# Graph layers on one core: three scatters to a slot, earlier SA loads, both message halves in one PSUM tile, later reloads of h

## Chip, core and metric

One NeuronCore of a Trainium2 chip runs one program. The metric is the device time of one execution in microseconds; several executions of a kernel are taken and their median is compared. Engines are named as in the profile: PE is TensorE (PEld its weight loads), DVE VectorE, ACT ScalarE, POOL GpSimd, SP SyncE. SP, ACT and POOL also issue DMAs; all of them run on the core's 16 DMA engines.

## What is computed

Two graph layers for 16 batches of 1024 nodes with 256 features, all in float32. `adj` is a 1024x1024 matrix with few nonzero edges.

```python
# layer 0, for each batch (feats = data @ W1.T, f1 = feats @ W2 + b2)
coefs = softmax(leaky_relu(f1[:, :, None] + f1[:, None, :]) + adj, axis=-1)
h = coefs @ feats + bias2 + data
# layer 1
hidden = relu(h @ W1u at u + h @ W1v at v + b1)        # for each pair u, v
S = sigmoid(hidden @ w2 + b2)                          # B x 1024 x 1024
a = einsum('buv,bud->bvd', S * adj, h)
m = einsum('uv,bud->bvd', adj, h) * h
z = beta1 * h + beta2 * (a @ Wa + ba) + beta3 * (m @ Wm + bm)
```

Where `adj` is zero, S is not needed. So the kernel computes S for the edges alone.

## The kernel before

**Dense part.** For each batch the attention of layer 0 gives h. From h come the two ends of an edge's hidden vector, `pu` and `pw` (tables in DRAM of 272 columns to a batch), the product `ha` = h Wa (DRAM), and the message branch: `message` (L1162) multiplies h by `adj` for one half of the nodes (512) and one half of the features (128, index h), 8 matmuls of 128x512 on a one-bank PSUM tile; `keep_message` (L1173) multiplies that on DVE by h transposed (`hT`) into `mT`; `product` (L1180) multiplies `mT` by Wm for two chunks of 128 nodes; `keep_product` (L1192) adds beta1 h into `zb`, and `store_product` (L1198) stores `zb` to DRAM from ACT's queue. Eight batches (LATER = 0, 1, 2, 3, 11, 12, 13, 14) put this branch off: their h goes to DRAM (`put_off`) and comes back through `take_up` (L1156), an SP load of 1 MB into one of three buffers `xh`; `turned_ends` then transposes h again on PE (`ph`), and ACT copies it to `hT`.

**Score part.** The batches are split into three groups with index 0, 1, 2 of 5, 5 and 6 batches. Each goes through 135 slots of 128 edges. `fetch` gathers a slot's rows of `pw` (tile `gv`) and, at the first slot of a table tile, of `pu` (tile `gu`) by indirect DMAs from POOL; `compare` (L1248) makes two DVE operations of it; `sums` (L1263) adds up each batch's 272 columns on ACT (every eighth slot of group 2 on DVE); after 16 slots ACT and DVE make the gates (`lg`), and each slot's gates are scattered to `sa_d` in DRAM by one more indirect DMA from POOL (`scatter`, L1232). Scatters whose gates are ready wait in the list `late`; `first` (L1283), at the head of every slot, fetches the slot some places ahead and then issues one or two scatters from that list. Group 0 and 1 have five buffers `gv`, group 2 has six of its own.

**Gather part.** When all of a group's scatters are done, `load_sa` (L1333) loads pieces of its `sa_d` on SP (tile `sat`, 7 buffers), ACT turns each round (`part_sa`, tile `apart`, 4 buffers), DVE multiplies it by `adj` (`weigh_sa`, L1354), and PE multiplies it by `ha` (`gather`, L1361, tiles `pzg` and `pzh`). `load_zb` brings `zb` back, DVE adds, ACT's queue stores the result. The groups are gathered in the order 1, 0, 2. So while group 2 is scored, PE does first what is left of the put-off messages and then the gathering of groups 1 and 0; group 2 is gathered at the end.

**Order.** No scheduler decides it: every step is put into a `Timetable` with a planned time (`times.at`; `times.matmuls` also advances the PE clock of the plan), and the steps are emitted in the order of those times. Each engine works through its own stream in that order and stops at the first instruction that must wait. DMAs of SP and ACT together use eight completion counters in turn, POOL's DMAs eight others: before a DMA is issued, its queue waits until the DMA eight places earlier in the same series has landed.

The put-off messages stand in a loop from L1617: seven times one `messages(..., 1)`, transposes, `messages(..., 0)`, two `product`s, so that `message`, `ph` and `pz` tiles all take turns in the four one-bank PSUM buffers `p1`; the two two-bank buffers `p2` are free meanwhile.

Of the kernel before, what the change touches and what calls it, by code (L numbers as in the profile page):

```python
# [8 lines left out]
F32 = mybir.dt.float32  # L9
AF = mybir.ActivationFunctionType  # L10
ALU = mybir.AluOpType
# [3 lines left out]
P = 128  # L15
BANK = 512
# [17 lines left out]
LATER = (0, 1, 2, 3, 11, 12, 13, 14)  # L34
# [337 lines left out]
def edge_layers(  # L372
# [36 lines left out]
    nc = tc.nc  # L409
    B, N, D = x.shape  # L410
    C = N // P
    H = D // P
    NG = len(GROUPS)
# [8 lines left out]
    p2 = ctx.enter_context(tc.tile_pool(name="p2", bufs=2, space=PSUM))  # L422
# [5 lines left out]
    adj_sb = const.tile([P, C, N], F32, name="adj_sb")  # L428
# [4 lines left out]
    dense = ctx.enter_context(tc.tile_pool(name="dense", bufs=1))  # L433
# [5 lines left out]
    held = {}  # L439
# [73 lines left out]
    for i in range(H):  # L513
# [5 lines left out]
        for o in range(H):  # L519
            nc.tensor.matmul(  # L520
                pw[:, :1],
                lhsT=w1_in[:, o, i * P : (i + 1) * P],
                rhs=w2_col0[:, o, :],
                start=(o == 0),
                stop=(o == H - 1),
# [397 lines left out]
    st = {}  # L923
# [232 lines left out]
    def take_up(b):  # L1156
        held[b] = dense.tile([P, C, D], F32, name="xh", bufs=3)
        nc.sync.dma_start(out=held[b].rearrange("p c d -> p (c d)"), in_=h_d[b])


    def message(b, half, h):
        span = slice(half * BANK, (half + 1) * BANK)  # L1162
        pm = st["pm", h] = p1.tile([P, BANK], F32, tag="p1", name="pm")
        for c in range(C):
# [5 lines left out]
                stop=(c == C - 1),  # L1170
            )

    def keep_message(b, half, h):  # L1173
        if h == 0:
            st["mT"] = dense.tile([P, H, BANK], F32, name="mT")
        nc.vector.tensor_tensor(
            st["mT"][:, h, :], st.pop(("pm", h)), st["hT", b, half][:, h, :], ALU.mult
        )
# [30 lines left out]
    PARTS = [16, 32, 48, 64, 80, 96, 112, 124, 131, len(SLOTS)]  # L1209
    AHEAD = [n - 2 for n in GV]  # L1210
    HA = 8
    SA = 7
    late = []

    def fetch(g, k):
        t, s = SLOTS[k]
        if s == 0:
            gu = st["gu", t] = pools["gath", g].tile([P, SIZE[g] * R], F32, name="gu", bufs=2)
            nc.gpsimd.indirect_dma_start(
                out=gu,  # L1220
                out_offset=None,
                in_=pu_d[g],
                in_offset=bass.IndirectOffsetOnAxis(ap=key_u[:, t : t + 1], axis=0),
            )
        gv = st["gv", k] = pools["gath", g].tile([P, SIZE[g] * R], F32, name="gv", bufs=GV[g])
        nc.gpsimd.indirect_dma_start(  # L1226
            out=gv,
            out_offset=None,
            in_=pw_d[g],
            in_offset=bass.IndirectOffsetOnAxis(ap=idx_v[:, t, s : s + 1], axis=0),  # L1230
        )

    def scatter(g, lg, i, k):
        t, s = SLOTS[k]
        dma = nc.gpsimd.indirect_dma_start(  # L1235
            out=sa_d[g],
            out_offset=bass.IndirectOffsetOnAxis(ap=idx_s[:, t, s : s + 1], axis=0),
            in_=lg[:, i, : SIZE[g]],
            in_offset=None,
            bounds_check=N * N - 1,  # L1240
            oob_is_err=False,
        )
        tc.declare_no_dep(dma.ins, group=f"sa{g}", reason="edges of their own")
        tc.add_to_no_dep_group(f"sa{g}", dma.ins)
# [4 lines left out]
    def compare(k, half):  # L1249
        if k in [0, *PARTS] and half == 0:  # L1250
            st["lg"] = dense.tile([P, PARTS[0], MOST], F32, name="lg", bufs=5)
        cols, op = ((slice(0, HALF), ALU.max), (slice(HALF, R), ALU.min))[half]
        mv = by_batch(st["gv", k])[:, :, cols]
        mu = by_batch(st["gu", SLOTS[k][0]])[:, :, cols]
        nc.vector.tensor_tensor(mv, mv, mu, op)  # L1255

    def place_of(k):

        part = next(i for i, end in enumerate(PARTS) if k < end)
        return (PARTS[part - 1] if part else 0), PARTS[part]  # L1260

    def sums(k, js, lg):
        one = by_batch(st["gv", k])  # L1263
        i = k - place_of(k)[0]
        if len(js) == one.shape[1]:
            nc.vector.tensor_reduce(lg[:, i, : len(js)], one, AX.X, ALU.add)
        else:
            for j in js:
                nc.scalar.activation(  # L1269
                    one[:, j, :], one[:, j, :], AF.Copy, accum_out=lg[:, i, j : j + 1]  # L1270
                )
# [7 lines left out]
    def scores(g, start, end, on_vector):  # L1279

        for k in range(len(SLOTS)):
            time = start + k * (end - start) / len(SLOTS)

            def first(k=k):
                for n in range(AHEAD[g]) if k == 0 else ():
                    fetch(g, n)
                if k + AHEAD[g] < len(SLOTS):
                    fetch(g, k + AHEAD[g])
                for _ in range(min(len(late), 2 if len(late) > PARTS[0] - 4 else 1)):
                    late.pop(0)()  # L1290

            def last(k=k):
                k0, k1 = place_of(k)
                lg = st["lg", k0]
                part = lg[:, : k1 - k0, : SIZE[g]]
                nc.vector.tensor_scalar(part, part, 1.0, None, ALU.add)
                late.extend(lambda i=i: scatter(g, lg, i, k0 + i) for i in range(k1 - k0))

            times.at(time - (15.0 if k == 0 else 0.0), first)
            times.at(time + 0.1, lambda k=k: compare(k, 0))  # L1300
            times.at(time + 0.9, lambda k=k: compare(k, 1))
            k0, k1 = place_of(k)
            if k == k0:
                times.at(time + 0.2, lambda k0=k0: st.update({("lg", k0): st["lg"]}))
            summed = lambda js, k=k, k0=k0: sums(k, js, st["lg", k0])
            if on_vector(k):
                times.at(time + 1.7, lambda f=summed: f(range(SIZE[g])))
            else:
                for j in range(SIZE[g]):
                    times.at(time + 2.0 + 0.6 * j, lambda f=summed, j=j: f((j,)))  # L1310
            if k + 1 == k1:
                times.at(time + 5.4, lambda k=k, k0=k0: gates(g, k, st["lg", k0]))
                times.at(time + 6.0, last)
        ended = end + 4.0
        if g + 1 == NG:
            times.at(ended, lambda: [late.pop(0)() for _ in range(len(late))])
        return ended
# [124 lines left out]
    def turned_ends(b, i):  # L1442
        end = times.matmuls(4 * P, lambda: turn_h(b, i))
        times.at(end + 0.3, lambda: keep_hT(b, i))
# [14 lines left out]
    def messages(b, half, h, delay=0.3):  # L1459
        time = times.matmuls(C * BANK, lambda: message(b, half, h))  # L1460
        times.at(time + delay, lambda: keep_message(b, half, h))

    def products(b, *ids):
        for i in ids:
            time = times.matmuls(4 * D, lambda i=i: product(b, i))
            times.at(time + 0.3, lambda i=i: keep_product(b, i))
            times.at(time + 2.3, lambda i=i: store_product(b, i))
        return time + 1.0

    times = Timetable()  # L1470
# [144 lines left out]
    times.at(lead - 0.5, check)  # L1615
    times.at(lead - 0.4, turn_over)
    messages(B - 1, 0, 1)  # L1617
    messages(B - 1, 1, 0, 3.8)
    products(B - 1, 0, 1)
    b = B - 1  # L1620
    for n in range(3):
        messages(b, 1, 1)
        turned_ends(LATER[n], 0)
        turned_ends(LATER[n], 1)
        messages(LATER[n], 0, 0, 3.8)
        time = products(b, 2, 3)
        b = LATER[n]
        times.at(time + 1.0, lambda b=LATER[n + 2]: take_up(b))
        messages(b, 0, 1)
        turned_ends(b, 2)  # L1630
        turned_ends(b, 3)
        messages(b, 1, 0, 3.8)
        products(b, 0, 1)
    messages(b, 1, 1)


    order = [*range(1, NG - 1), 0, NG - 1]
# [21 lines left out]
    for i, at in starts.items():  # L1659
        if i == 5:  # L1660
            continue
        b = LATER[i]
# [6 lines left out]
    when = []  # L1669
    begins = {}  # L1670
# [17 lines left out]
    due = when[last] - 30.0  # L1688
# [22 lines left out]
    )  # L1711
    for i, at in starts.items():
        if i + 2 < len(LATER):
            times.at(when[at] + 2.0, lambda b=LATER[i + 2]: take_up(b))
    times.at(when[starts[6]] + 2.0, load_rest)
    for n, (g, c) in enumerate((g, c) for g in order for c in range(C)):
        if n < C:
            due = opened + 2.0 + (when[0] - 14.0 - opened) * n / C
        elif n < HA:
            due = when[2 + n - C] + 0.1  # L1720
        else:
            k, c1 = divmod(n - HA, C)
            due = begins[order[k], C - 1, c1] + 2.4
        times.at(due, lambda g=g, c=c: load_ha(g, c))
    parts = list(begins)
    for i, p in enumerate(parts):
        due = when[0] - 36.0 + 4.0 * i if i < SA else begins[parts[i - SA]] - 4.0
        if p[0] + 1 == NG:
            due = max(due, ended + 0.1 + 0.01 * i)
        times.at(due, lambda p=p: load_sa(*p))  # L1730
        times.at(begins[p] - 8.2, lambda p=p: part_sa(*p))
        times.at(begins[p] - 6.0, lambda p=p: weigh_sa(*p))
    for i, (g, vc, half) in enumerate(halves):
        if half == 0:
            due = when[0] - 20.0 + 8.0 * i if i < 4 else when[i - 2] + 13.0
            if g + 1 == NG:
                due = max(due, ended + 0.2)
# [62 lines left out]
```

## Time and profile before

| | us |
|---|---|
| runs | 2083.23, 2078.31, 2081.45 (median 2081.45) |
| the profiled execution, its own time | 2079.83 |
| its span, first to last instruction | 2078.1 |
| PE busy | 2020.4 (97%) |
| DVE busy | 1566.8 (75%) |
| ACT busy | 1371.5 (66%) |
| POOL busy | 1142.4 (55%) |
| TensorE clock granted, mean | 0.994 |

The time is 1.7 us more than the span. All times given as places below are microseconds from the span's start. The put-off messages of the loop run from 1279 to 1416; PE then gathers groups 1 and 0 until 1904 and group 2 until 2069. POOL's last scatter stands at 1891. "Busy" PE is matmuls in the pipeline; idle time is what is left.

### The profile page before, as it was taken

Reading aid. Unit: us, or ns where it says so; the run is one execution under the profiler, and the core shown is the slowest. Engines: PE = TensorE matmul, PEld = TensorE weight load, DVE = VectorE, ACT = ScalarE, POOL = GpSimd, SP = SyncE. Lnnn points to the kernel's source line nnn. Section 1 sums busy time; section 2 is a strip of 40 time slices with the busy share of each in tenths; the row PEclk is TensorE's granted clock in tenths of the full one; section 3 lists DMA queues with packets and bytes.
Section 4 is the critical chain, followed back from the end, with each engine's and each line's share of the span. In section 5 each row is a group of like instructions: output and inputs, shape, how many; then the busy total and the mean of one; then the engine's idle time right before and its main releaser. Section 6 shows DMA issues by size and latency. Waiting matters only on the chain.

```text
span 2078.1 us, 28958 instructions
## 1 busy us (share of the span) xinstructions
PE 2020.4 (97%) x8577; PEld 1554.9 (75%) x8577; DVE 1566.8 (75%) x2348; ACT 1371.5 (66%) x4842; POOL 1142.4 (55%) x974
## 2 busy tenths in 40 slices
PE   8999999999999999999999999899999999999998
PEld 6888887777786868677888886457677667767887
DVE  7798883677777777677878886578888888884554
ACT  4212222577777868587888777577888888885654
POOL 1121221267676777677777777666777677683000
PEclk9999999999999999999999999999999999999999
DMA  6689886788888889789999999999999999996873
GB/s 220 240 311 343 306 323 235 247 268 288 285 273 270 275 288 297 254 299 308 315 297 318 327 308 310 326 401 399 399 400 370 415 414 405 400 383 254 281 230 123
DMA packets 250007, 644.37 MB, mean 310 GB/s; under 512 B 38642, under 2 KB 139762, under 8 KB 247794
## 3 DMA queue, kind: packets, MB, share of 16 engines
q0 software_dynamic: 82016, 348.87, 47.9%
q1 hardware_dynamic: 132002, 259.36, 34.2%
q10 hardware_dynamic: 35824, 34.22, 4.7%
q8 instruction: 69, 1.13, 0.2%
q14 instruction: 96, 0.79, 0.1%
HBM read 479.56 MB, written 162.92 MB: 309 GB/s over the span
## 4 chain that ended last, share of the span: by engine, by line
PE 61%; DVE 11%; DMA 9%; ACT 8%; issue 7%; POOL 3%; ACTq 0%; POOLq 0%; DVEq 0%
PE pv L1067 18%; PE pp L1105 10%; PE pm L1165 10%; PE pzg L1370 6%; DMA gv<-pw_d,idx_v 5%; ACT gv L1269 5%; PE pf L1013 5%; DVE gv L1255 4%; PE pea L1133 4%; PE pzh L1370 3%; PE pz L1185 2%; ACT apart L1352 2%; POOL sa_d L1235 2%; DMA xh<-in_x_dram 1%; POOL gv L1226 1%
## 5 line engine op out<-in xcount | busy, mean ns | idle before, releaser
L1269 ACT ACTIVATE gv<-gv 128x272 f32<-128x272 f32 x2058 | 856.3, 420 | 313.0 <-DVE gv L1255 204.7
L1255 DVE TENSOR_TENSOR gv<-gv,gu 128x680 f32<-128x680 f32 (+1 forms) x810 | 705.8, 909 | 97.5 <-DMA gv<-pw_d,idx_v 95.5
L1226 POOL DMA_INDIRECT gv<-pw_d,idx_v x405 | 497.1, 1227 | 297.9 <-ACT gv L1269 181.5
L1235 POOL DMA_INDIRECT sa_d<-lg,idx_s x405 | 504.1, 1245 | 135.2 <-issue 108.2
L1067 PE MATMUL pv<-feats,eT 128*128 128x257 f32 x2048 | 465.5, 380 | 2.7 <-DVE eT L1054 2.0
L1165 PE MATMUL pm<-adj_sb,xh 128*128 128x512 f32 x1024 | 452.8, 595 | 2.6 <-DVE xh L1081 2.6
L1067 PEld LDWEIGHTS pv<-feats,eT 128*128 128x128 f32 x2048 | 382.9, 190 | 61.8 <-DVE eT L1054 4.2
L1269 ACT ACTIVATION_READ_ACCUMULATOR gv<-gv 128x1 f32 x2058 | 389.7, 189 | 0.0
L1370 PE MATMUL pzg<-ha_g,apart 128*128 128x256 f32 x1536 | 367.5, 382 | 19.0 <-DVE apart L1357 18.5
L1165 PEld LDWEIGHTS pm<-adj_sb,xh 128*128 128x128 f32 x1024 | 194.3, 191 | 222.4 <-issue 219.8
L1370 PEld LDWEIGHTS pzg<-ha_g,apart 128*128 128x128 f32 x1536 | 290.2, 191 | 77.2 <-DVE apart L1357 29.5
L1352 ACT COPY apart<-sat 128x640 f32<-128x640 f32 (+1 forms) x192 | 264.2, 1394 | 78.0 <-PE pzh L1370 35.5
L1357 DVE TENSOR_TENSOR apart<-apart,adj_sb 128x640 f32<-128x640 f32 (+1 forms) x192 | 165.9, 867 | 123.3 <-ACT apart L1352 123.0
L1105 PE MATMUL pp<-wuv,hT 128*128 128x272 f32 x1024 | 250.5, 395 | 6.7 <-ACT end L1119 3.8
L1105 PEld LDWEIGHTS pp<-wuv,hT 128*128 128x128 f32 x1024 | 194.7, 191 | 53.7 <-issue 6.5
L1054 DVE SCALAR_TENSOR_TENSOR eT<-row,col,grown 128x512 f32<-128x512 f32 x256 | 182.8, 745 | 27.5 <-ACT col L1000 26.8
L852 POOL DMA_INDIRECT table_d<-rec,at x52 | 57.4, 1105 | 248.4 <-DVE rec L845 151.8
L1098 ACT COPY hT<-ph 128x512 f32<-128x512 f32 x96 | 55.1, 575 | 101.0 <-PE ph L1087 100.7
L1133 PE MATMUL pea<-wa,hT 128*128 128x256 f32 x512 | 121.0, 379 | 0.0
L1185 PE MATMUL pz<-wm,mT 128*128 128x256 f32 x512 | 115.7, 379 | 0.0
L1013 PE MATMUL pf<-w1T,xT 128*128 128x257 f32 x512 | 114.1, 380 | 0.9 <-DVE xT L971 0.9
L1370 PE MATMUL pzh<-ha_g,apart 128*128 128x256 f32 x384 | 114.2, 379 | 0.0
(179 smaller groups left out, 1589.0 us busy)
## 6 DMA issues: line engine op xcount, KB each, us to landing
sa_d<-zero SPq DMA_DIRECT2D x128, 512.0 KB, 5.6
sat<-sa_d SPq DMA_DIRECT2D x128, 320.0 KB, 9.5
sat<-sa_d SPq DMA_DIRECT2D x64, 384.0 KB, 4.2
pu_d<-end SPq DMA_DIRECT2D x64, 272.0 KB, 4.3
pw_d<-end SPq DMA_DIRECT2D x64, 272.0 KB, 5.8
ha_d<-ea SPq DMA_DIRECT2D x64, 256.0 KB, 4.9
zb_d<-zb ACTq DMA_DIRECT2D x64, 256.0 KB, 7.8
xh<-in_x_dram SPq DMA_DIRECT2D x15, 1024.0 KB, 13.6
```

The costliest lines, as they stand in the source:

```text
L1013: nc.tensor.matmul(pfs[i], lhsT=st["xT"][:, h, c * P : (c + 1) * P], rhs=w1T[:, h, :], start=(h == 0), stop=(h == H - 1),)
L1054: nc.vector.scalar_tensor_tensor(st["eT", b, k, n][:, i, :], st["row"][:, cols], st["col"][:, j : j + 1], grown[:, j, cols], ALU.max, ALU. ...
L1067: nc.tensor.matmul(pv[:, : D + 1], lhsT=st["eT", b, k, j // 4][:, j % 4, i * P : (i + 1) * P], rhs=st["feats", b][:, j, :], start=(j == 0) ...
L1105: nc.tensor.matmul(pp[:, k, :R], lhsT=st["hTi", b, i][:, h, k * P : (k + 1) * P], rhs=wuv[:, side, h, :], start=(h == 0), stop=(h == H - 1),)
L1133: nc.tensor.matmul(pp[:, k, :], lhsT=st["hTi", b, i][:, h, k * P : (k + 1) * P], rhs=wa[:, h, :], start=(h == 0), stop=(h == H - 1),)
L1165: nc.tensor.matmul(pm, lhsT=held[b][:, c, h * P : (h + 1) * P], rhs=adj_sb[:, c, span], start=(c == 0), stop=(c == C - 1),)
L1226: nc.gpsimd.indirect_dma_start(out=gv, out_offset=None, in_=pw_d[g], in_offset=bass.IndirectOffsetOnAxis(ap=idx_v[:, t, s : s + 1], axis=0),)
L1235: dma = nc.gpsimd.indirect_dma_start(out=sa_d[g], out_offset=bass.IndirectOffsetOnAxis(ap=idx_s[:, t, s : s + 1], axis=0), in_=lg[:, i, : ...
L1255: nc.vector.tensor_tensor(mv, mv, mu, op)
L1269: nc.scalar.activation(one[:, j, :], one[:, j, :], AF.Copy, accum_out=lg[:, i, j : j + 1])
L1352: nc.scalar.copy(apart.rearrange("p g v -> p v g"), sat)
L1370: nc.tensor.matmul(st["pzg", g, vc][j // 4][:, j % 4, :], lhsT=apart[:, j, :], rhs=ha, start=(c == 0 and j % 2 == 0), stop=(c == C - 1 and ...
```

## The change

Four edits, all around the change from group 1's scores to group 2's.

1. **Scatters.** In the first 16 slots of group 2, `first` issues up to three scatters from `late` to a slot, where it issued one (two while the list is long). What is in the list then are the last 18 scatters of group 1. In the program as built, POOL's stream behind group 2's first five `gv` gathers was: one scatter, group 1's last `gu` and `gv`, 4 scatters, a gather, 2, a gather, and then one scatter to each gather up to the 18th. It is now: 3 scatters, group 1's last `gu` and `gv`, 4, a gather, 3, a gather, 3, a gather, 3, `gu` and a gather, 2, and then gathers alone.
2. **Messages.** In the loop both feature halves of a message go into one two-bank tile `pms` of `p2` (`message_pair`, 16 matmuls) and are taken out by one DVE operation over 1024 columns (`keep_pair`). Each half now runs: transposes of the next half, its message pair, then the products of the half before it, and then `keep_pair`. The matmuls are the same in number and shape. The transposes stand in front of the message pair rather than between its two parts.
3. **Reloads.** The `take_up` of the batches gathered along with the groups is planned 8 us instead of 2 us after the PE step that it follows.
4. **SA loads.** The first seven `load_sa` are planned 10 us earlier. In SP's stream the first now stands after the fourth load of `ha`, and the seven take turns with the last four loads of `ha`; before, the first stood behind the sixth. The load of the fifth put-off h now stands behind the seven, where it stood behind the fourth. ACT's stream carries the stores of `zb` at other places, and the two stores of batch 1's first half now use the completion counters that the first two SA loads use.

```diff
+    def message_pair(b, half):
+        span = slice(half * BANK, (half + 1) * BANK)
+        pm = st["pms", b, half] = p2.tile([P, H, BANK], F32, tag="p2", name="pms")
+        for h in range(H):
+            for c in range(C):
+                nc.tensor.matmul(
+                    pm[:, h, :],
+                    lhsT=held[b][:, c, h * P : (h + 1) * P],
+                    rhs=adj_sb[:, c, span],
+                    start=(c == 0),
+                    stop=(c == C - 1),
+                )
+
+    def keep_pair(b, half):
+        st["mT"] = dense.tile([P, H, BANK], F32, name="mT")
+        nc.vector.tensor_tensor(
+            st["mT"], st.pop(("pms", b, half)), st["hT", b, half], ALU.mult
+        )
...
-                for _ in range(min(len(late), 2 if len(late) > PARTS[0] - 4 else 1)):
+                most = 2 if len(late) > PARTS[0] - 4 else 1
+                if g + 1 == NG and k < PARTS[0]:
+                    most = 3
+                for _ in range(min(len(late), most)):
                     late.pop(0)()
...
     messages(B - 1, 0, 1)
-    messages(B - 1, 1, 0, 3.8)
-    products(B - 1, 0, 1)
-    b = B - 1
-    for n in range(3):
-        messages(b, 1, 1)
-        turned_ends(LATER[n], 0)
-        turned_ends(LATER[n], 1)
-        messages(LATER[n], 0, 0, 3.8)
-        time = products(b, 2, 3)
-        b = LATER[n]
-        times.at(time + 1.0, lambda b=LATER[n + 2]: take_up(b))
-        messages(b, 0, 1)
-        turned_ends(b, 2)
-        turned_ends(b, 3)
-        messages(b, 1, 0, 3.8)
-        products(b, 0, 1)
-    messages(b, 1, 1)
+    parts = [(b, half) for b in (B - 1, *LATER[:3]) for half in range(2)]
+    for n, (b, half) in enumerate(parts[1:]):
+        if b != B - 1:
+            turned_ends(b, 2 * half)
+            turned_ends(b, 2 * half + 1)
+        times.matmuls(2 * C * BANK, lambda b=b, half=half: message_pair(b, half))
+        b1, half1 = parts[n]
+        time = products(b1, 2 * half1, 2 * half1 + 1)
+        times.at(times.now + 0.35, lambda b=b, half=half: keep_pair(b, half))
+        if half1:
+            times.at(time + 1.0, lambda b=LATER[n // 2 + 2]: take_up(b))
...
-            times.at(when[at] + 2.0, lambda b=LATER[i + 2]: take_up(b))
+            times.at(when[at] + 8.0, lambda b=LATER[i + 2]: take_up(b))
...
-        due = when[0] - 36.0 + 4.0 * i if i < SA else begins[parts[i - SA]] - 4.0
+        due = when[0] - 46.0 + 4.0 * i if i < SA else begins[parts[i - SA]] - 4.0
```

## The prediction, made before the changed kernel had run

> **What bounds the kernel now.** The first view is PE's waits over the whole span, since PE is busy 97%.
>
> ```profile
> PE pzg L1370 <- DVE apart L1357: 18.5, 23, 2.9
> PE ph L1087 <- DVE zb L1195: 8.7, 2, 7.3
> ```
>
> Columns: total us, times, longest. PE idles 57.7 us in all (2078.1 less 2020.4); these two groups are the only ones above 4 us. The second belongs to the put-off messages. PE's timeline shows its full price:
>
> ```profile
> 1325.61 7.03 PE L1165 MATMUL pm<-adj_sb,xh 128*128 128x512 f32 x16
> 1339.92 1.12 PE L1087 MATMUL ph<-ident,xh 128*128 128x128 f32 x4 [7.28 <-DVE zb L1195]
> 1342.41 1.12 PE L1087 MATMUL ph<-ident,xh 128*128 128x128 f32 x4 [1.38 <-DVE zb L1195]
> 1343.32 8.29 PE L1165 MATMUL pm<-adj_sb,xh 128*128 128x512 f32 x16
> 1351.45 3.62 PE L1185 MATMUL pz<-wm,mT 128*128 128x256 f32 x16
> ```
>
> From the first of these matmuls to the `pz` it takes 25.84 us; the same sequence undisturbed (1354.91 to 1369.52) takes 14.61. The stall costs 11.2 us, of which 8.7 are idle and the rest a slower clock behind it. But does PE set the end? The chain of waits, near the end of the scores, says no:
>
> ```profile
> 1862.90 10.57 DMA gv<-pw_d,idx_v
> 1873.57 1.01 DVE gv L1255
> 1874.58 0.75 DVE apart L1357
> 1875.36 3.44 PE pzg L1370 x8
> ```
>
> From 1875 to 2069 the chain is PE without a gap; from 1295 to 1875 it runs mainly through gathers, POOL, DVE's compares and ACT's sums. PE only follows. Two more views back this up: in 1416 to 1880 neither DVE nor ACT is listed with any wait for PE, while PE keeps waiting a little for `apart`; and the windows show what the scores run against:
>
> ```profile
> 1325.00:1350.00 25.00, 16.34 (x41) 7.92 (x40) 14.51 (x18) 11.19 (x49) 13.56 (x13) 0.80 0.84 302
> 1375.00:1400.00 25.00, 25.00 (x79) 13.44 (x78) 19.08 (x23) 16.74 (x74) 12.91 (x12) 1.00 1.02 415
> 1400.00:1425.00 25.00, 24.25 (x83) 15.29 (x82) 17.07 (x20) 15.21 (x56) 13.66 (x13) 1.00 1.03 415
> ```
>
> Behind PE, PEld, DVE, ACT and POOL come the granted clock, the DMA share and GB/s. From about 1360 on the 16 DMA engines are full: at 415 GB/s, a gather of 0.836 MB costs 2.0 us, a load of `ha` 1.6, of h 2.5, of an SA piece 0.8. So from here to the first gathers on PE the scores can gain only what the DMA engines lose before 1360.
>
> **The change, part by part.**
>
> *Messages.* What held PE was DVE, stuck on group 1's last gather:
>
> ```profile
> 1319.01 1.65 DVE L1255 TENSOR_TENSOR gv<-gv,gu 128x680 f32<-128x680 f32 x2 [2.86 <-DMA gv<-pw_d,idx_v]
> 1334.71 3.48 DVE L1255 TENSOR_TENSOR gv<-gv,gu 128x680 f32<-128x680 f32 x4 [14.05 <-DMA gv<-pw_d,idx_v]
> 1339.12 0.75 DVE L1195 SCALAR_TENSOR_TENSOR zb<-xh,be,pz 128x512 f32<-128x512 f32 x1
> ```
>
> That wait stays. With the pair in `p2` PE needs DVE later: from 1279.06, one half is 13.9 (a pair, as the row 1640.93 has it) + 3.45 (`pz`) + 0.88 (`ph`) = 18.2; three halves and a pair end at 1347.6, where the next `pz` wants `mT`. DVE, free at 1334.7, has in front of it in the new order: 1.7 (slot 134), 1.9 (slot 0), until 1339.1 for the gates, 3.8 (two slots), two `zb` of 0.75 with a compare of 1.0, and the pair, 1.2 by the nearest row of 1024 columns (`zg<-zg,pzg`, 1216 ns): done at 1346.6. So the stall of 11.2 shrinks to between 0 and 3; I take 1. DVE saves 7 instructions, under 1 us. PE would reach its first `pzg` at 1405.8 instead of 1415.96. There it meets the scores: the first `apart` stands on DVE right behind slot 20's compares (1410.56 before), the third came at 1419.48, done 1420.3, and PE began on it at 1420.36. PE had no slack there. What it wins at 1332 it waits for at 1406 to 1420, unless the scores come earlier. Term: 0; if the cover were gone and PE did bind, -10.
>
> *Scatters.* Twelve more scatters (three rather than one to a slot) go in front of gathers, each 1.01 plus 0.30 on POOL:
>
> ```profile
> 1334.15 0.98 POOL L1235 DMA_INDIRECT sa_d<-lg,idx_s  x1 [0.30 <-issue]
> 1341.65 0.98 POOL L1226 DMA_INDIRECT gv<-pw_d,idx_v  x1 [6.51 <-ACT gv L1269]
> 1345.04 1.52 POOL L1226 DMA_INDIRECT gv<-pw_d,idx_v  x1 [0.30 <-issue]
> ```
>
> Two before group 1's last gather make its issue 2.6 late; but the queue before it lands only at 1331.3, so it still lands near 1334.6 (0 to 2.6 late). Three fit in the 6.51 that POOL waits for ACT. The gathers of slots 7, 8 and 9 go out 2.6, 5.2 and 6.5 later (1359.6 for slot 9), then POOL has no scatters and has caught up at slot 13. DVE took slot 9 at 1367.39 after 1.05 of waiting: 14.3 us after its issue, behind an h and four `ha` loads. Now one `ha` load is in front; gathers land 6.1 us after issue (median of 1300 to 1345) to 11.4 (of 1350 to 1420):
>
> ```profile
> gv<-pw_d,idx_v POOLq DMA_INDIRECT x12, 6.1
> ```
>
> That gives 1365.7 to 1371.0, -1.6 to +3.7 for the scores; I take +1, nearer the crowded row. The last scatter goes out at 1358 instead of 1380.01, and the first SA load, which waited for it until 1388.85, at about 1367 (8.8 us landing, as before).
>
> *SA loads and reloads.* The seven SA loads (5.7 us of DMA) and four `ha` loads (6.3) move by some 20 us against each other. All of them must be in before PE's fourth piece either way, so with full DMA engines nothing is won or lost in sum. What moves is a wait on ACT:
>
> ```profile
> ACT gv L1269 <- DMA sat<-sa_d: 6.5, 1, 6.5
> ```
>
> At 1411 to 1417 a `zb` store on ACT waited for its completion counter, held by the SA load issued at 1399.03; all sums stood behind it. In the new order this store's counter is free (-6.5), but the two stores of batch 1's first half now wait for the first two SA loads to land. ACT comes to them at about 1371 and 2 us later; the loads land 7.0 and some 10 after issue (1388.85 to 1395.87 and 1399.01), at 1374 and 1377: 3 + 1 more, bounds 0 and 14. I take +5.5 with both, net -1. Queued behind: the sums, so POOL's next gathers. The later `take_up` takes 2.8 us of waiting for `zb` (1431.7 to 1434.5) out of SP's stream, where seven SA buffers were full: 0; without that cover -2.8.
>
> The Trainium skill, "DMA: Bandwidth & Descriptors", section "Issuing engines are not separate DMA queues", says that DMAs of all issuers interleave on the same 16 engines; the landing of a gather in 6.1 us alone and 11.4 beside SP's loads agrees. By that rule alone, loads brought forward by 20 us push the gathers back by their own 5.7 us, and the sum would be 2085; by the rows, the later loads they displace make way for gathers again. The same page (section "Where 436 GB/s comes from") has a limit of about 358 GB/s for HBM on a core; the trace holds 415, so the measurement decides.
>
> **Sum**, on the profiled execution's 2079.83: 0 (messages) + 1 (scatters) - 1 (waits on ACT) = 2079.8, so 2080. The median of the runs is 1.6 above that execution; the two can't be told apart from one another, since about 0.2%, or 4.2 us, is what a measurement here can tell.
>
> **Rivals.**
>
> *Faster: the scores do gain.* In 1340 to 1416 DVE waited for PE 14.5 us (`zb` 10.0, `mT` 4.5); with PE ahead that goes, and so does the 6.5 on ACT. For it: behind 1425 the DMA engines carry 388 to 405 GB/s for 175 us, 5% or 9 us below 415, room in which a lead is kept. Against: between 1360 and 1425 they have none. Price 8, between 6.5 and 9: 2072 (2068 to 2075).
>
> *Slower: ACT stands still for the first SA loads.* It decides if the last scatter of group 1 lands after 1364, 7 us before ACT reaches the store. At 1375 both stores cost 8 + 3 = 11 less 6.5, and slots 7 to 9 come up to 3.7 late: +6 to +8, 2086. For it: DMA is full there, and the scatters' landing stretched to 8.8. Against: SP's stream is short of loads then.
>
> *The stall stays.* If `mT` is late by the waits of ACT's gates or of slots 1 and 2, PE still idles 7 us near 1348. As PE is ahead of the scores then, the time is that of the forecast, 2080.
>
> **How the numbers follow.** Forecast 0.36, faster 0.35, slower 0.23, stall stays 0.06. Likeliest is no change, 2080, its own range 2076 to 2084 (4.2 to each side). The range of all reaches into both rivals, 2070 to 2087. Faster by over 0.2%: 0.35, within: 0.36 + 0.06 = 0.42, slower: 0.23.
>
> **What would show it.** Right: `ph <- zb` gone from PE's waits, `pzg <- apart` grown by 6 to 10 us, most of it before 1425; DVE's 14 us for the last gather of group 1 still there; first SA load issued near 1367; `sa_d`'s last scatter of group 2 within 4 us of 1891. Wrong: that last scatter earlier by more (the scores gained), or a wait of ACT of 8 us or more near 1371 that moves it later. If the end moved while that scatter stayed, the reading of the chain was wrong.

## The result, and the profile after

| | us |
|---|---|
| before, 12 runs | 2081.53 median (2076.33 to 2083.23) |
| after, 12 runs | 2086.53 median (2082.85 to 2088.36) |
| ratio after to before | 1.0026, 95% interval 1.0017 to 1.0035 |
| after, the profiled execution | 2086.71, its span 2085.0 (before 2079.83 and 2078.1) |

The changed kernel is slower by 0.26%, just over what can be told apart. No change was forecast.

The view read first before the change was PE's waits (total us, times, longest). After:

```profile
PE pzg L1392 <- DVE apart L1379: 24.4, 26, 4.5
PE pzg L1392 <- issue: 4.6, 1, 4.6
...
PE pz L1204 <- DVE mT L1188: 3.7, 3, 2.1
```

The two waits of `ph` for `zb`, 8.7 us, are gone; PE's waits for `apart` are 24.4 us where they were 18.5. PE's timeline at the place of the old stall:

```profile
1333.86 13.90 PE L1178 MATMUL pms<-adj_sb,xh 128*128 128x512 f32 x32
1348.94 3.69 PE L1204 MATMUL pz<-wm,mT 128*128 128x256 f32 x16 [1.18 <-DVE mT L1188]
1352.47 1.04 PE L1087 MATMUL ph<-ident,xh 128*128 128x128 f32 x8
```

Of the 11.2 us at this place 1.18 are left. So the message edit does what it says. The chain of waits, at the place where PE took over from the scores:

```profile
1868.14 12.14 DMA gv<-pw_d,idx_v
...
1880.37 1.01 DVE gv L1274
1881.38 0.75 DVE apart L1379
1882.17 3.22 PE pzg L1392 x8
```

The last gather of the scores still hands over to PE, only 5.2 us later (1862.90 before), and POOL's last scatter of group 2 goes out at 1896.73 instead of 1891.21. All but 1.4 of the 6.9 us that the span grew is in the stream of scores. The windows (PE, PEld, DVE, ACT, POOL busy, granted clock, DMA share, GB/s) say the same of PE:

```profile
1325.00:1350.00 25.00, 23.82 (x72) 12.69 (x72) 11.87 (x15) 10.85 (x49) 14.67 (x15) 1.00 0.87 325
1375.00:1400.00 25.00, 24.52 (x72) 12.59 (x71) 16.37 (x18) 14.60 (x67) 10.73 (x8) 1.00 1.02 417
1400.00:1425.00 25.00, 16.32 (x56) 10.89 (x54) 21.14 (x25) 20.22 (x75) 15.47 (x13) 0.93 1.02 415
```

PE is 7.5 us busier in the first row than before and 7.9 less busy in the third: it came early and waited. From 1375 to 1425 the DMA engines are as full as they were. What became later is to be seen on DVE, at the wait for group 1's last gather, and on POOL behind it:

```profile
1317.61 1.63 DVE L1274 TENSOR_TENSOR gv<-gv,gu 128x680 f32<-128x680 f32 x2
1337.35 3.48 DVE L1274 TENSOR_TENSOR gv<-gv,gu 128x680 f32<-128x680 f32 x4 [18.11 <-DMA gv<-pw_d,idx_v]
```

```profile
1349.52 1.05 POOL L1245 DMA_INDIRECT gv<-pw_d,idx_v  x1 [0.30 <-ACT gv L1288]
1350.87 0.99 POOL L1254 DMA_INDIRECT sa_d<-lg,idx_s  x1 [0.30 <-issue]
1352.16 1.21 POOL L1254 DMA_INDIRECT sa_d<-lg,idx_s  x1 [0.30 <-issue]
1353.68 1.52 POOL L1254 DMA_INDIRECT sa_d<-lg,idx_s  x1 [0.30 <-DVE gv L1274]
1355.50 1.54 POOL L1238 DMA_INDIRECT gu<-pu_d,key_u  x1 [0.30 <-issue]
1357.34 1.51 POOL L1245 DMA_INDIRECT gv<-pw_d,idx_v  x1 [0.30 <-issue]
```

The wait is 18.11 us (14.05 before) and ends at 1337.35 (1334.71). The gather at 1357.34 is that of slot 8; three scatters and a `gu` stand between it and the one before. It went out at 1349.68 before. The first reading was that the scatters had done both. The runs show that they did only the second.

### The profile page after: what moved, and what is told of

It is laid out like the page before. It is cut to its first block, busy times and chain, and to the rows that moved or that the text cites. A ratio compares the mean times of both kernels' runs of the same rounds, so it can differ in the third digit from the quotient of the medians.

```text
span 2085.0 us, 28955 instructions
## 1 busy us (share of the span) xinstructions
PE 2022.3 (97%) x8577; PEld 1558.8 (75%) x8577; DVE 1566.1 (75%) x2341; ACT 1371.7 (66%) x4842; POOL 1129.4 (54%) x974
## 4 chain that ended last, share of the span: by engine, by line
PE 55%; DVE 16%; DMA 12%; ACT 8%; issue 6%; POOL 3%; ACTq 0%; DVEq 0%; POOLq 0%; SPq 0%
PE pv L1067 16%; PE pp L1105 8%; PE pm L1165 8%; DMA gv<-pw_d,idx_v 7%; DVE gv L1274 7%; PE pzg L1392 6%; ACT gv L1288 5%; PE pf L1013 4%; PE pea L1133 4%; PE pzh L1392 3%; ACT apart L1374 2%; PE pz L1204 2%; DVE eT L1054 1%; POOL sa_d L1254 1%; DMA out_dram<-zg 1%
## 5 line engine op out<-in xcount | busy, mean ns | idle before, releaser
L1245 POOL DMA_INDIRECT gv<-pw_d,idx_v x405 | 484.7, 1197 | 305.6 <-ACT gv L1288 188.5
L1392 PE MATMUL pzg<-ha_g,apart 128*128 128x256 f32 x1536 | 369.1, 384 | 29.5 <-DVE apart L1379 24.4
L1165 PE MATMUL pm<-adj_sb,xh 128*128 128x512 f32 x800 | 351.4, 593 | 1.7 <-DVE xh L1081 1.7
L1165 PEld LDWEIGHTS pm<-adj_sb,xh 128*128 128x128 f32 x800 | 151.5, 190 | 171.8 <-issue 169.6
```

The lines of the kernel that those rows point to most:

```text
L1165: nc.tensor.matmul(pm, lhsT=held[b][:, c, h * P : (h + 1) * P], rhs=adj_sb[:, c, span], start=(c == 0), stop=(c == C - 1),)
L1245: nc.gpsimd.indirect_dma_start(out=gv, out_offset=None, in_=pw_d[g], in_offset=bass.IndirectOffsetOnAxis(ap=idx_v[:, t, s : s + 1], axis=0),)
L1392: nc.tensor.matmul(st["pzg", g, vc][j // 4][:, j % 4, :], lhsT=apart[:, j, :], rhs=ha, start=(c == 0 and j % 2 == 0), stop=(c == C - 1 and ...
```

## The experiments

All ratios are to the kernel before, run beside on the same chip. "Gathers" are POOL's `gv` gathers of the scores in order of issue. The 271st is group 2's second (its first where group 1's last gather goes ahead of them), and from the 276th on the numbers mean the same slot in every kernel: the 277th is slot 6 of group 2, the 405th the last.

| kernel | ratio | 95% interval | MB moved in 1310 to 1365 |
|---|---|---|---|
| before | 1 | | 18.8 |
| changed kernel, first time and again | 1.0026, 1.0037 | 1.0017 to 1.0035, 1.0023 to 1.0050 | 16.7, 16.4 |
| without sooner SA loads | 1.0025 | 1.0015 to 1.0034 | 17.1 |
| without later reloads | 1.0026 | 1.0015 to 1.0037 | 16.9 |
| scatters and SA loads only | 1.0014 | 1.0005 to 1.0022 | 16.8 |
| scatters only | 1.0012 | 1.0003 to 1.0020 | 17.1 |
| message pairs only | 0.9990 | 0.9981 to 0.9999 | 18.6 |
| changed kernel, third h held back | 1.0022 | 1.0013 to 1.0032 | 17.2 |
| last gather first | 0.9979 | 0.9970 to 0.9988 | 20.7 |
| last gather first, pairs | 0.9991 | 0.9980 to 1.0003 | 19.5 |
| last gather first, pairs, third h held back | 0.9976 | 0.9965 to 0.9987 | 20.4 |

The last column is 55 us times the GB/s of a window 1310 to 1365 of each profile; the rows of six kernels stand below.

The eight runs of the first and the fourth set are not in the table. They ran on two chips, called disturbed below, where before itself took 2103.39 and 2115.52 us and scattered by 1%; there the 271st gather went out at 1332 to 1361 rather than 1313 to 1319, so the edits met another stretch.

### First set: the suspects one by one

Scatters alone (the kernel before with the first edit):

```diff
-                for _ in range(min(len(late), 2 if len(late) > PARTS[0] - 4 else 1)):
+                most = 2 if len(late) > PARTS[0] - 4 else 1
+                if g + 1 == NG and k < PARTS[0]:
+                    most = 3
+                for _ in range(min(len(late), most)):
```

> The kernel before with the first edit alone: three scatters to a slot in group 2's first 16 slots; messages, reloads and the plan of the SA loads as before. Theory S (the scatters cost the time, because twelve of them stand before gathers): 4 to 7 us slower than before, 2085 to 2088; DVE's longest wait for a gather near 1335 is 16 us or more (14.05 before); POOL's last scatter of the last group 4 to 7 us later than before. Rival L (the sooner SA loads cost it): within 2 us of before, 2080 to 2083. Rival M (the message order costs it): the same, 2080 to 2083.

Measured 1.0005 (0.9987 to 1.0022), on a disturbed chip: no loss is seen there, but the interval reaches 4.6 us.

Scatters undone (the changed kernel without that edit):

> The changed kernel with its first edit undone: one scatter to a slot (two while the list is long), the other three edits kept. Theory S: the loss goes, 2079 to 2083, DVE's wait for group 1's last gather back to 13 to 15 us, although the first SA load cannot go before the last scatter, at about 1385 to 1389. Rival L or M: the loss stays, 2085 to 2088. Theory S would also be held back if the SA loads, planned early and waiting in SP's stream for the last scatter, made the loads of ha behind them late; then PE waits for ha before 1450.

Measured 1.0026 (1.0005 to 1.0046), on the same chip. It decides nothing: the planned-early SA loads stood in SP's stream before their scatters were done, the case named at the end of the expectation. SP issued the first at 1407 and the next at 1416 to 1425, and DVE's longest wait for a gather between 1420 and 1480 was 11.5 us.

Message pairs alone (the kernel before with the second edit, the loop as in the diff above):

> The kernel before with the second edit alone: both halves of a put-off message in one PSUM tile. Theory S with PE as follower: PE's 7.3 and 1.4 us waits for zb near 1340 go, its waits for apart grow by 6 to 10 us, time within 2 us of before, 2080 to 2083. Rival M: 4 to 7 us slower, 2085 to 2088. Rival P (PE does set the end): 6 to 11 us faster, 2070 to 2075.

Measured 0.9984 (0.9965 to 1.0002): not slower, and not the gain of rival P.

Group 1's last gather first:

```diff
-            times.at(time - (15.0 if k == 0 else 0.0), first)
+            times.at(time - (13.0 if k == 0 else 0.0), first)
```

> The kernel before with one other edit: the first six gathers of group 2 are planned 2 us later, which puts group 1's last two gathers (gu and gv of its last slot) in front of them and of one scatter on POOL; nothing else moves. Theory S, whose core is that DVE's wait for that one gather sets where the stream of scores starts: the wait of 14.05 us shrinks to 5 or less, POOL's last scatter comes 4 to 10 us sooner, 2071 to 2078. Rival D (the full DMA engines behind 1360 swallow any lead): POOL's last scatter within 2 us, 2079 to 2083.

Measured 0.9987 (0.9972 to 1.0003).

### Second set: one edit taken back

The first is the changed kernel again. The second takes back the fourth edit and the last one the third:

```diff
-        due = when[0] - 46.0 + 4.0 * i if i < SA else begins[parts[i - SA]] - 4.0
+        due = when[0] - 36.0 + 4.0 * i if i < SA else begins[parts[i - SA]] - 4.0
```

```diff
-            times.at(when[at] + 8.0, lambda b=LATER[i + 2]: take_up(b))
+            times.at(when[at] + 2.0, lambda b=LATER[i + 2]: take_up(b))
```

The third is the kernel before with the scatters of the first set and `when[0] - 46.0`.

> The changed kernel once more, unaltered, beside the three below on one chip, since the chip of the first four runs was another 1% slower and scattered by 1%. If its loss is its own and not the chip's: ratio to before 1.001 to 1.004 as at first. If it is 1.000 or less, the loss depends on when the stream of scores meets the rest, and only stretches of the profiles can be compared.

> The changed kernel with the SA loads planned as before (10 us later), the other three edits kept. Rival L (the sooner SA loads cost the time: seven loads and their waits fall among the gathers of slots 14 to 20): 4 to 6 us faster than the changed kernel, within 1 us of before or faster. Theory S (the scatters cost it): as the changed kernel, within 1.5 us. From the 271st gather of the scores to the last one (547.9 us before, 552.5 in the changed kernel): L gives 545 to 549, S gives 551 to 554.

> The kernel before with the scatters three to a slot and the SA loads sooner; messages and reloads as before. Rival L: the loss of the changed kernel is there, 3 to 6 us above before, and 551 to 554 from the 271st gather to the last. If neither edit costs by itself but only together with the message pairs (Theory C, the SA loads meet a PE that runs ahead): within 2 us of before, 546 to 549.

> The changed kernel with the reloads of h planned as before, 2 us rather than 8 us after the step they follow. If the later reloads cost the time (Theory R: they push h into later gathers): 3 to 6 us faster than the changed kernel. By S, L and C: within 1.5 us of the changed kernel.

Measured 1.0037, 1.0025, 1.0014, 1.0026; from the 271st gather to the last 553.8, 552.0, 551.0 and 552.6 us (547.9 before). The loss is the kernel's own. Taking back the SA loads or the reloads wins 0 to 2.5 us, nothing that the intervals can tell from none: neither explains the loss, rivals L and R fall as its main cause. The last kernel differs from the third by the pairs alone: 2.5 us by the ratios, 3.2 by the medians (2085.16 and 2081.98), with intervals that overlap; with the later reloads too it is 4.8 (1.0037 against 1.0014), and there they just do not; but those of the changed kernel's first 12 runs (1.0026) do. Theory S alone does not foresee that.

### Third set: scatters, pairs and the early gather on a quiet chip

The first three are kernels of the first set; the fourth has the early gather's one line and the pairs of the third.

> The scatters alone once more, since the chip of the first four runs ran their stream of scores 16 to 38 us late and the edit met another stretch. Theory S (gathers of slots 7 to 9 go out late behind three scatters each, the DMA engines run dry near 1340 to 1360, and that service is lost for good): 2 to 5 us slower than before; from the 271st gather to the 286th 60 to 61.5 us, where it was 57.2 before and 59.9 to 61.1 in the four runs that had the edit. Theory M2 (the pairs cost most of it): within 1.5 us.

> The message pairs alone once more. Theory S: within 1.5 us of before, 57 to 58 us from the 271st gather to the 286th. Theory M2 (the pairs cost most of the loss, since PE, no longer held, brings its DVE, ACT and DMA work into the stretch where the gathers are short): 2.5 to 5 us slower.

> Group 1's last gather ahead of group 2's first once more. By theory S the lost service before 1360 is what counts, and DVE's wait of 14 us for that gather is its cause: the wait shrinks to 5 or less, the DMA engines get gathers sooner between 1330 and 1360, 3 to 8 us faster, 2072 to 2077. By rival D (the lead is lost again where the SA loads and reloads crowd the engines): within 1.5 us.

> Group 1's last gather first, and the message pairs. If the scores set the end alone, as the run with the gather alone, within 1.5 us. If with the wait gone PE's stall near 1340 becomes the bound, the pairs win another 2 to 6 us on top. If the pairs cost by themselves (M2), 2.5 to 5 us slower than with the gather alone.

Measured 1.0012, 0.9990, 0.9979, 0.9991. The scatters alone cost 2.4 us (0.6 to 4.2), with 61.7 us from the 271st to the 286th gather, just above what S had. The pairs alone gain 2 us (0.2 to 4.0), against M2, though that stretch took 60.0 us and not 57 to 58. The early gather alone gains 4.4 us (2.5 to 6.2) and beats both kernels; with the pairs beside it 2.5 us of that are lost (3.5 by the medians, with intervals that overlap). So the pairs gain alone, and beside scatters or beside the early gather they cost by the medians each time, but within the intervals.

Why the wait of DVE grew: its row in the run with scatters alone, then in that with pairs alone.

```profile
1334.27 3.48 DVE L1255 TENSOR_TENSOR gv<-gv,gu 128x680 f32<-128x680 f32 x4 [14.10 <-DMA gv<-pw_d,idx_v]
```

```profile
1336.49 3.48 DVE L1274 TENSOR_TENSOR gv<-gv,gu 128x680 f32<-128x680 f32 x4 [18.28 <-DMA gv<-pw_d,idx_v]
```

With 3 scatters in front the last gather lands no later than before; with the pairs it lands 2 us later although it was issued sooner (`gu` in front of it at 1321.11, with scatters 1324.41). SP's timeline shows what got between, first before, then after:

```profile
1309.14 0.35 SPq L1158 DMA_DIRECT2D xh<-h_d  x1
```

```profile
1316.59 0.35 SPq L1158 DMA_DIRECT2D xh<-h_d  x1
```

This is the reload of the third put-off h, 1 MB or 2.5 us of all DMA engines. It waits for a buffer that the last products of batch 15 free. With pairs, half a message more stands before those products on PE, so the load goes out 7 us later, right among the gathers of 1313 to 1323.

Where the bytes went: the window 1310 to 1365 before, after, with scatters alone, with pairs alone and with the early gather.

```profile
1310.00:1365.00 55.00, 46.34 (x137) 24.82 (x136) 31.37 (x39) 30.71 (x135) 37.15 (x34) 0.91 0.92 342
```

```profile
1310.00:1365.00 55.00, 53.82 (x168) 29.53 (x167) 29.59 (x36) 30.17 (x136) 38.27 (x36) 1.00 0.86 304
```

```profile
1310.00:1365.00 55.00, 47.10 (x139) 25.24 (x138) 28.68 (x36) 29.89 (x131) 40.58 (x37) 0.91 0.84 311
```

```profile
1310.00:1365.00 55.00, 53.63 (x168) 29.50 (x167) 33.89 (x40) 31.65 (x143) 34.48 (x33) 1.00 0.92 338
```

```profile
1310.00:1365.00 55.00, 55.00 (x171) 30.18 (x171) 33.20 (x41) 33.57 (x148) 37.88 (x34) 1.00 0.97 377
```

Read the last number. A reckoning made after the runs: at the full rate of 415 GB/s, the 38 GB/s that the changed kernel lacks for 55 us (2.1 MB) are 5.0 us; the 31 of the scatters 4.1; the 4 of the pairs 0.5; the 35 that the early gather has more are -4.6. Measured were +5.4 and +7.7, +2.4, -2.1 and -4.4. In all eleven profiles of the table this reckoning comes within 2.7 us of the measured ratio. That separates the losing kernels from the gaining ones, but not the losing ones from each other: they moved 299 to 313 GB/s and measured +2.4 to +7.7. It is also no law that what the DMA engines miss here is missed to the end. In the profile with scatters alone the 286th gather went out 4.2 us later than before, the 316th 2.1, the last 0.6, and the span was 0.2 longer, where the reckoning says 4.1; after the change the same gathers were 3.6, 5.4 and 5.2 us late. Against the spans of the same profiles the reckoning errs by up to 3.9 us. The early gather shows a gain, by its place on POOL and what DVE then does:

```profile
1312.81 0.96 POOL L1219 DMA_INDIRECT gu<-pu_d,key_u  x1 [0.30 <-issue]
1314.08 0.94 POOL L1226 DMA_INDIRECT gv<-pw_d,idx_v  x1 [0.30 <-DMA zb_d<-zb]
```

```profile
1323.18 1.64 DVE L1255 TENSOR_TENSOR gv<-gv,gu 128x680 f32<-128x680 f32 x2 [1.99 <-DMA gv<-pw_d,idx_v]
1327.19 1.93 DVE L1255 TENSOR_TENSOR gv<-gv,gu 128x816 f32<-128x816 f32 x2 [2.37 <-issue]
```

The last gather of group 1 (128x680) is compared at 1323 rather than 1335, and group 2's first slot follows at 1327 rather than 1336; PE has no stall near 1340 in this run, without any change to the messages. Its 4.4 us hold both, DVE's shorter wait and PE's missing stall; the pairs, which take away the stall alone, won 2.

### Fourth and fifth set: the third h held back

The load is taken out of the loop and planned behind the first load of `ha`:

```diff
-        if half1:
+        if half1 and n > 1:
             times.at(time + 1.0, lambda b=LATER[n // 2 + 2]: take_up(b))
...
     opened = paced[NG - 1] + 7.0
+    times.at(opened + 2.05, lambda: take_up(LATER[2]))
```

The second kernel is before with scatters and pairs, the third and fourth hold the load back behind the early gather, with and without pairs.

> The changed kernel with one reload elsewhere: the third put-off h (1 MB), which SP issues at 1316 in every kernel with the pairs and at 1309 in every one without, is planned behind the first load of ha, so near 1342. Theory H (the pairs free that buffer 7 us later, so that this load falls among group 2's first gathers and group 1's last one; it is why DVE's wait for that gather is 17.2 to 18.3 us with the pairs and 14.1 without): the wait is back to 13 to 15.5, the load goes into the stretch 1340 to 1360 where the DMA engines run half empty, 3 to 5 us faster than the changed kernel, ratio to before 1.0003 to 1.0012. If the load isn't the cause: wait 17 to 18, within 1.5 us of the changed kernel.

> The kernel before with scatters and message pairs, SA loads and reloads as before. If the two stack only as their single runs did (+2.4 and -1.9 us): within 1.5 us of before. If they cost together what the changed kernel costs (both starve the DMA engines in the same stretch, 1336 to 1364, so that what the pairs win is lost and more): 4 to 6 us slower, 59.5 to 61.5 us from the 271st gather to the 286th.

> Group 1's last gather first, the message pairs, and the third put-off h behind the first load of ha. By theory H the 3.5 us that the pairs cost on top of the early gather go: 2071 to 2075 where before stands at 2079.6, ratio 0.996 to 0.998. If not H: as the early gather with the pairs, 0.999.

> Group 1's last gather first and the third put-off h behind the first load of ha, messages as before. By theory H the load leaves the stretch of the early gathers here too: 0 to 3 us faster than the early gather alone, ratio to before 0.9965 to 0.998. If the h then comes too late for PE's transposes: PE waits for xh before 1380, and the gain is gone.

Measured 1.0040 (1.0013 to 1.0068), 1.0040 (1.0009 to 1.0071), 1.0019 (0.9992 to 1.0045) and 1.0019 (0.9994 to 1.0044), on the second disturbed chip, the first, third and fourth not as theory H had it. Scatters and pairs together cost 0.40% there, where their single runs on the other disturbed chip add up to -0.11%. But every kernel of this set that also ran on a quiet chip, as it is or in a close form, comes out 0.2 to 0.4% worse here (the fourth 1.0019, the early gather alone 0.9979), so this does not yet show that the two cost together. The first and the third were run again, on a quiet chip:

> The changed kernel with the third put-off h behind the first load of ha once more, since the chip of the four runs before ran its stream of scores 30 us late. Theory H: DVE's wait for group 1's last gather 13 to 15.5 us (17.2 to 18.3 with the pairs so far, 14.1 without), service that the DMA engines lose between the 271st and the 277th gather 3 to 5.5 us (5.9 to 7.1 with the pairs, 4.8 to 5.2 without), ratio to before 1.0005 to 1.0015, where the changed kernel has 1.0026 to 1.0037. If the reload isn't the cause: wait 17 to 18, ratio 1.002 to 1.004.

> Group 1's last gather first, message pairs, and the third put-off h behind the first load of ha, once more. Theory H: ratio to before 0.996 to 0.998, where the early gather alone has 0.9979 and the early gather with the pairs 0.9991. If not H: 0.9985 or more.

Measured 1.0022 (1.0013 to 1.0032) and 0.9976 (0.9965 to 0.9987). DVE's row in the first:

```profile
1338.43 3.48 DVE L1274 TENSOR_TENSOR gv<-gv,gu 128x680 f32<-128x680 f32 x4 [14.91 <-DMA gv<-pw_d,idx_v]
```

The row ends later than in the changed kernel (1337.35) because the whole stream ran some 3 us late in this execution. Counted from the 271st gather's issue, DVE begins this compare after 19.9 us; it is 21.4 to 22.6 in the five profiles with pairs and the reload in its old place, and 19.6 to 19.7 in before and the two without pairs. So the reload was the cause of the longer wait, as H said. But it was worth 1 to 3 us at most in the changed kernel, within the intervals, where H had 3 to 5; and the service lost from the 271st to the 277th gather (the stretch less the packets in it, each at the lower quartile of its size's durations, over 16 engines) was 7.0 us against a foreseen 3 to 5.5. With the early gather the ratio that H foresaw came: 0.9976, where the pairs without this edit had 0.9991 (the intervals still overlap), and the window 1310 to 1365 moves 370 GB/s:

```profile
1310.00:1365.00 55.00, 55.00 (x171) 30.23 (x170) 35.15 (x41) 35.64 (x160) 39.30 (x35) 1.00 0.97 370
```

The early gather alone (0.9979) and this (0.9976) can't be told apart. Both beat the kernel before by 4 to 5 us, neither has the scatters, the sooner SA loads or the later reloads.

## Why the prediction missed

- *What bounds the kernel.* Right. Taking PE's 11 us stall away won 2 us alone; moving one gather of the scores by 10 us won 4.4 without touching PE's program. In both the gain is in the scores: their last gather goes out at 1860.76 and 1857.86, before at 1862.90. After the change group 2's last scatter came 5.5 us later, outside the 4 that the prediction allowed, though no wait of ACT of 8 us stood near 1371.
- *Messages, the stall.* Right: forecast to shrink to between 0 and 3, 1 taken; 1.18 measured. PE arrived at 1409.8 (forecast 1405.8) and waited there, `pzg <- apart` grew by 5.9 and one wait of 4.6 beside it.
- *Messages, "that wait stays" and the term 0.* Wrong. The wait grew to 17.2 to 18.3 us in the five profiles with pairs in which neither that gather nor the reload was moved. The prediction counted DVE's instructions of the moved step, but not the DMA that its products release: the third reload. Alone the term was -2; beside the scatters it was a loss.
- *Scatters, +1 taken, -1.6 to +3.7.* The two in front of group 1's last gather were read rightly: it lands at 1334.27. Slots 7 to 9 were to go out 2.6, 5.2 and 6.5 late; with scatters alone they went out 2.9, 6.3 and 7.5 late (1347.93, 1355.94, 1360.52). The price was taken where DVE receives the gathers. By the bytes that the engines did not move, the prediction's own rule of "what the DMA engines lose before 1360", it is +4.1; measured +2.4 (0.6 to 4.2), inside the bounds, and the value taken lies in the interval too.
- *SA loads: "nothing is won or lost in sum".* Right within the intervals: 1.0025 without that edit, 1.0026 and 1.0037 with it. *Waits on ACT, -6.5 and +5.5.* Neither shows in the time. ACT's waits for `sat` in 1360 to 1420 are gone after, but ACT waits for DVE instead:

```profile
ACT gv L1288 <- DVE gv L1274: 18.7, 6, 4.9
```

  before it was 9.9 us beside the 6.5. The two stores came to ACT at 1383.87 and 1384.53, not 1371, and no load held them up. And with scatters alone the 6.5 went as well, without any sooner plan: the last scatter was sooner, and the loads followed it. There too ACT waited for DVE instead, 18.2 us.
- *The step that failed* is the sum. Messages 0, scatters +1 and waits on ACT -1 were added as if independent. The single runs of scatters and messages, +2.4 and -2.1, do add up to the forecast of no change; together, with the other two edits, they cost 5.4 and 7.7, and with edit 3 or edit 4 taken back still 5.4 and 5.2 (1.0026 and 1.0025). The sum had no term for what scatters and pairs cost beside each other, 5 us or more. Both do press on the gathers issued from 1313 to 1360: the scatters push them back on POOL, the reload takes their place on the DMA engines. But that alone does not explain the 5 us. From the 271st gather to the 286th the kernels with both take no longer than the one with scatters alone; the difference comes behind it. In us between the issues of the gathers:

| kernel, profiled execution | 271st to 286th | 286th to 316th | 316th to last |
|---|---|---|---|
| before | 57.2 | 121.2 | 369.5 |
| scatters only | 61.7 | 119.1 | 368.1 |
| message pairs only | 60.0 | 118.5 | 367.7 |
| both, with edit 3, edit 4 or both (five profiles) | 59.1 to 61.1 | 122.9 to 123.1 | 368.6 to 369.8 |

  From the 286th gather to the 316th each edit alone wins back 2 to 3 us; together they lose 2 more. (On the disturbed chips it was 119.1, 118.7 and, with scatters and pairs but neither edit 3 nor 4, 123.8; but the early gather alone, 118.8 on the quiet chip, took 124.6 there.) The windows of that stretch before, after, with scatters alone and with pairs alone:

```profile
1372.21:1493.39 121.18, 119.87 (x442) 80.51 (x441) 96.51 (x111) 94.62 (x338) 82.95 (x63) 1.00 1.02 404
```

```profile
1375.84:1498.82 122.98, 111.03 (x410) 75.61 (x409) 98.52 (x112) 98.27 (x352) 80.71 (x60) 0.99 1.02 405
```

```profile
1376.36:1495.44 119.08, 117.14 (x435) 79.31 (x434) 99.17 (x115) 97.76 (x352) 80.46 (x61) 1.00 1.03 411
```

```profile
1374.55:1493.04 118.49, 111.54 (x411) 76.02 (x410) 94.53 (x108) 94.83 (x340) 82.89 (x63) 0.99 1.02 406
```

  The DMA engines are full in all four. After the change they move 49.8 MB in this stretch, where it was 49.0 before and 48.9 and 48.1 with the single edits, and 19.7 MB in the stretch ahead of it, where it was 20.2, 20.2 and 21.3. So about 1 MB or more of other transfers, 2.5 us at 405 GB/s, came behind the 286th gather, and with scatters alone the rate is higher too. Over all three stretches every one of the four moves 216 MB. The single edits catch up; the two together do not.
- *The rivals.* The time of the slower one, 2086, was right and its mechanism was not: ACT did not stand still for SA loads. The faster one named DVE's 14.5 us of waiting for PE in 1340 to 1416. They did go, but DVE waits for gathers instead. In that window these waits were 1.3 us before; after the change:

```profile
DVE gv L1274 <- DMA gv<-pw_d,idx_v: 18.7, 7, 6.5
```

  Nor did the changed kernel win anything in the room behind 1425: from the 316th gather to the last it took 369.3 us, before 369.5.

*Left open.* Scatters and pairs without the rest have not been run on a quiet chip, nor the changed kernel without its scatters in a form in which no SA load waits. The reload explains the longer wait; beside the early gather its move wins back by the ratios what the pairs lost, with intervals that overlap. Why the single edits win back behind the 286th gather what they lost ahead of it, and the two together do not, was not found; each row of the gathers' table but the last is one execution.

## What to carry over

Where a shared resource is full for a long stretch, an edit ahead of it can be priced by the work that the resource no longer gets done there (bytes by full rate) and not only by the delay of one consumer. Here that gave the sign for ten kernels of eleven, their sizes only within 2.7 us, and with scatters alone 4 us that were behind at one place were nearly all won back by the end of the stage. So it is a first estimate, and the last transfer of the stage is what decides. A wait whose length is set by one transfer issued behind others can be mended by the order of issue, here by one constant. Two edits that draw on one resource need a run of both: here each alone was worth about 2 us, one up and one down, and together, with the other two edits, they cost 5 or more. When a step moves, follow the buffers it frees: the transfer that waits for them moves too, here by 7 us.

## What the runs showed of the hardware

With eight DMAs of POOL outstanding, each further issue in this program waits for the one eight places before: with pairs alone, three scatters and a gather stood 1.87, 1.29, 1.35 and 1.06 us for gathers to land, so a small scatter can hold POOL up for as long as the large gathers ahead of it need. One kernel differs more between chips than these edits are worth: before took 2079.55 to 2081.53 us on four occasions and 2103.39 and 2115.52 on two; the profiles taken there agree within 1 us at the first gather (357) and are 17 to 46 us late at the 271st. Most of that loss lies in the scores of groups 0 and 1 (with the early gather alone 20.7 of 30.1 us), so a small edit behind them is better judged where that does not happen.
